# Queries and keys of the first spatial attention beside the end of the layers' last item, with the layers' pools on two sides of the memory

## The chip, the cores and the metric

The kernel runs on one core of a Trainium2 chip. The metric is device time in microseconds (us), the median of three runs. A core has five engines that each work through their own queue in order: TensorE (PE; its weight loads are PEld), VectorE (DVE), ScalarE (ACT), GpSimd (POOL) and SyncE (SP), which issues most of the DMAs. An engine that waits for a semaphore holds up everything behind it in its queue. SBUF holds the tiles the engines work on, PSUM the results of TensorE.

## The reference

The input is `x` of shape 2 x 128 x 64 x 64 in float32. Four blocks follow each other:

- **Layers.** A 1x1 embedding, two layers of layer norm, a selective state-space scan with gate, and a two-step feed-forward network with gelu, then a 1x1 output projection and the residual.
- **First spatial attention.** Queries, keys and values come from three 3x3 convolutions of the layers' output; softmax over all 4096 positions; a 1x1 projection; the residual.
- **Second spatial attention.** The same with 1x1 projections.
- **Multi-scale fusion.** 3x3 convolutions of the image at four scales, a small attention over the four scales at each pixel, a layer norm, and a fusion to 128 channels.

```python
q = conv2d(x, Wq, bq, 1).reshape(b, c, n)
k = conv2d(x, Wk, bk, 1).reshape(b, c, n)
v = conv2d(x, Wv, bv, 1).reshape(b, c, n)
attn = softmax(einsum('bci,bcj->bij', q, k) * scale, axis=2)
out = einsum('bij,bcj->bci', attn, v)
```

## The kernel before

The image lies in SBUF all the time as `xt`, with 128 channels on the partitions and both batches with a border of zeros. All blocks read it and write it back in place. Each block is a `with` body of its own that opens its tile pools at the start and closes them at the end. The order of the instructions on every engine is the order in which the Python code emits them (`tc.manual_schedule()`).

**Layers (L108 to L531).** The work is cut into `NI` = 32 items: 2 batches x 2 layers x 8 chunks of 512 positions, batch 0 first. An item has 32 slots. A loop runs `i` from -2 to 33, and in each slot it emits the scan's part (`spread_dt`, `spread_dtu`, `y_pair`, `scan`, `decay`, `times_b`, by groups of four slots, 256 groups in all) and then what `background(i)` lists for the slot. `background(i)` mixes four items at different stages: item `i+2` enters (embedding, first layer norm), `i+1` gets its projections, `i` its gate input, `i-1` ends its scan (`y_out` L407, `gate` L410, `mix_out` L416 to L420, second layer norm L222 to L278, `ffn_up` L429), and `i-2` ends with `gelu` L433, `ffn_down` L441 to L443, `ffn_add` L449 and L450, `out_mm` L455 and L456, `out_add` L460.

For `i` = 32 and 33 there is nothing left to scan after the slot 7 of item 32. What remains is the end of item 30 (L441 to L460) and the chain of the last item, 31: L407, L410, L416, L417, L420, L222 (centre), L229 (square), L236 (variance), L240 (`ve`), L244 to L247 (`rs`, `nt` on ScalarE), L252, L253, L257 (a Newton step on GpSimd and ScalarE), L261 (`pr`, the factor spread over the partitions), L265 (`cen`, on VectorE), L278 (`x2`, on ScalarE), L429 and L430 (four times), gelu, L441 to L460.

Pools of the layers: `l0w` (weights), `l0s` (all working tiles, among them five `h` tiles of 8 KB per partition, `bb`, `cb`, `dt`, `dtu`, `dtb`, `u`, `z`, `carry`), and in PSUM `l0mm` (2 banks), `l0bc` (1), `l0da` (4), `l0y` (1). `hid`, the feed-forward network's middle, uses the `h` tiles.

**First attention.** Runs `r` = 0 to 3 are (first, second attention) x (batch 0, 1). The pool `wbig` gets the weights `wa` (L539) and `uw`, a ring of three half filter sets (L573, 576 KB each) beside the tile `dlo`. The 3x3 convolutions of the first attention are computed in a transformed form. A batch's rows are cut into four chunks. For one chunk, `inputs` (L589 to L600) makes twelve VectorE combinations of shifted columns, eight into `dlo`, four into `dhi`; `products` (L612) multiplies them in six slots of three matmuls each into `pa` and `pb`; `outputs` copies two parts on ScalarE (L561, L620) and combines nine times on VectorE (L621 to L629). At the start of run 0 the queries of chunk 0 and the keys of all four chunks (`keys`) are made, in this order; then the loop over `now` begins, with scores (L706, taken up by VectorE's L711), exponentials (L721), transposes (L736), block copies and DMAs (L743, L745, L747) and products (L756).

A pool that is opened where closed pools lay waits, at its first uses, for the last user of those pools.

**Multi-scale.** It opens with the weights `ws` (L874), a few weight products (L890 to L907) and the image's means (L948).

Of the kernel before, what the change touches and what calls it, by code (L numbers as in the profile page):

```python
# [67 lines left out]
def tile_conv_seq(ctx: ExitStack, tc, x, consts, vecs, wemb, wlay, wconv, wdt, wqkv, wsmall, wms, out):  # L68
# [42 lines left out]
    with ExitStack() as s, tc.manual_schedule():  # L111
        wp = s.enter_context(tc.tile_pool(name="l0w", bufs=1))
        sp = s.enter_context(tc.tile_pool(name="l0s", bufs=1))
        mm = s.enter_context(tc.tile_pool(name="l0mm", bufs=2, space=PSUM))
        bc = s.enter_context(tc.tile_pool(name="l0bc", bufs=1, space=PSUM))
        dap = s.enter_context(tc.tile_pool(name="l0da", bufs=4, space=PSUM))
        yp = s.enter_context(tc.tile_pool(name="l0y", bufs=1, space=PSUM))
# [106 lines left out]
        def ln_square(w, k, i):  # L224
            if "sq" not in w:
                w["sq"] = sp.tile([P, 2, CH], F32, name="sq", tag="sq")
                w["cen"] = sp.tile([P, 2, CH], F32, name="cen", tag="cen")
            pc = w.pop(("pc", k))
            nc.scalar.activation(w["sq"][:, k, :], pc, AF.Square)  # L229
            nc.scalar.copy(w["cen"][:, k, :], pc)  # L230
# [7 lines left out]
        def ln_eps(w, n):  # L238
            w["ve"] = sp.tile([2, CH], F32, name="ve", tag="ve")
            nc.scalar.activation(w["ve"][:n], w.pop("var")[:n], AF.Identity, bias=eps[:n])  # L240

        def ln_rs(w, n):
            w["rs"] = sp.tile([2, CH], F32, name="rs", tag="rs")
            nc.scalar.activation(w["rs"][:n], w["ve"][:n], AF.Ln)  # L244
            nc.scalar.activation(w["rs"][:n], w["rs"][:n], AF.Exp, scale=-0.5)
            w["nt"] = sp.tile([2, CH], F32, name="nt", tag="nt")
            nc.scalar.activation(w["nt"][:n], w["rs"][:n], AF.Square)  # L247
# [19 lines left out]
        def ln_shift(w, k, i, second):  # L267
            if second:
                dst = st[i]["x2"] = sp.tile([P, CH], F32, name="x2", tag="x2")
# [26 lines left out]
        def pz_mm(i, j):  # L296
            if j == 0:
                st[i]["z"] = sp.tile([P, NJ, CH], F32, name="z", tag="z", bufs=2)
# [124 lines left out]
        def ffn_up(i, f):  # L423
            w = st[i]
            if f == 0:
                w["hid"] = sp.tile([P, 4, CH], F32, name="hid", tag="h", bufs=5)
# [18 lines left out]
        def ffn_add(i):  # L445
            b, l, c = items[i]
            if l == NL - 1:
                xr = st[i]["xr"] = sp.tile([P, CH], F32, name="xr", tag="xr")
# [65 lines left out]
        for i in range(-2, NI + 2):  # L514
            todo = background(i)
            for t_ in range(NSL):
                t = i * NSL + t_
                g, m = divmod(t, 4)
                if m == 0 and 0 <= g + 3 < NG:
                    spread_dt(g + 3)  # L520
                if m == 0 and 0 <= g + 1 < NG:
                    spread_dtu(g + 1)
                if m == 0 and g % 2 == 1 and 0 <= g - 3 < NG:
                    y_pair(g - 3)
                if 0 <= t < NT:
                    scan(t)
                if 0 <= t + 4 < NT:
                    decay(t + 4)
                if m == 3 and 0 <= g + 1 < NG:
                    times_b(g + 1)  # L530
                for f, a in todo[t_]:  # L531
                    f(*a)


    wbig = ctx.enter_context(tc.tile_pool(name="wbig", bufs=1))
    wa = wbig.tile([P, NWA], F32, name="wa")

    uw = wbig.tile([P, NS, 9, C], F32, name="uw", tag="wbig")
    nc.sync.dma_start(wa, wsmall[:, :NWA])  # L539
# [3 lines left out]
    QG = 256  # L543
    NB, NTH = P // 32, N // P // 2
    NU = 8 * N // QG
    LAG = 14
    with ExitStack() as s, tc.manual_schedule():
        sp = s.enter_context(tc.tile_pool(name="ats", bufs=1))
        pss = s.enter_context(tc.tile_pool(name="atps", bufs=2, space=PSUM))
        psa = s.enter_context(tc.tile_pool(name="atpa", bufs=2, space=PSUM))  # L550
        psm = s.enter_context(tc.tile_pool(name="atpm", bufs=1, space=PSUM))
        psq = s.enter_context(tc.tile_pool(name="atpq", bufs=1, space=PSUM))
# [5 lines left out]
        st = {}  # L558
# [11 lines left out]
        def load(which, half):  # L570
            slot = st["ring"] = (st.get("ring", -1) + 1) % 3
# [5 lines left out]
        def inputs(r, cc):  # L577

            dhi = st["dhi"] = sp.tile([P, 2, 18, 16], F32, name="dhi", tag="d")
# [23 lines left out]
        def products(which):  # L603
# [3 lines left out]
            for slot, dst in enumerate((pa[:, 2, :], pa[:, 0, :], pa[:, 3, :], pa[:, 1, :], pb[:, 0, :], pb[:, 1, :])):  # L607
                d = dlo[:, slot] if slot < 4 else st["dhi"][:, slot - 4]
                for y in range(3):
                    rhs = d[:, y : y + 16, :].rearrange("p h j -> p (h j)")  # L610
                    lhsT = uw[:, where[which, slot // 3], 3 * (slot % 3) + y, :]
                    nc.tensor.matmul(dst, lhsT=lhsT, rhs=rhs, start=(y == 0), stop=(y == 2))  # L612
            return pa, pb

        def outputs(pa, pb, dst, bias):

            tt, stt = nc.vector.tensor_tensor, nc.vector.scalar_tensor_tensor
            df = sp.tile([P, 2, QG], F32, name="df", tag="df")
# [37 lines left out]
        def keys(r):  # L656
            k = st["k"] = sp.tile([P, N], F32, name="k", tag="k")
            chunks(r, 1, lambda cc: k[:, cc * 4 * QG : (cc + 1) * 4 * QG])

        def values(r):  # L660
            vt = st["vt"] = sp.tile([P, N // P, C], F32, name="vt", tag="vt")
# [11 lines left out]
            def to(cc):  # L673
                if cc > 1:
                    turned(cc - 2)
                vs[cc] = sp.tile([P, 4 * QG], F32, name="vs", tag="tr", bufs=2)
# [6 lines left out]
        def queries(r, cc):  # L683

            for i in range(4):
                st["q", r, 4 * cc + i] = sp.tile([P, QG], F32, name="q", tag="q", bufs=5)
            outputs(*products(0), [st["q", r, 4 * cc + i] for i in range(4)], bias(r, 0))

        def query(r, grp):
            ps = psq.tile([P, QG], F32, name="pqq", tag="q")  # L690
            dense(r, 0, grp * QG, QG, ps)
            q = st["q", r, grp] = sp.tile([P, QG], F32, name="q", tag="q", bufs=5)
# [3 lines left out]
        def score(r, u):  # L696
            grp, w = divmod(u, 8)
            it, c2 = divmod(w, 4)
            if c2 == 0:
                st["mx"] = sp.tile([P, NCH // 2], F32, name="mx", tag="mx", bufs=2)  # L700
            if c2 % 2 == 0:
                st["sc", r, u // 4, c2 // 2] = sp.tile([P, N // 2], F32, name="sc", tag="sc", bufs=3)
            pq = pss.tile([P, 2, CH], F32, name="pq", tag="s")
            for i in range(2):
                at = (2 * c2 + i) * CH
                nc.tensor.matmul(  # L706
                    pq[:, i, :], lhsT=st["q", r, grp][:, it * P : (it + 1) * P], rhs=st["k"][:, at : at + CH], start=True, stop=True
                )
            at = c2 % 2 * 2 * CH
            dst = st["sc", r, u // 4, c2 // 2][:, at : at + 2 * CH].rearrange("p (a f) -> p a f", a=2)  # L710
            nc.vector.tensor_scalar(dst, pq, 1.0, None, ALU.mult, ALU.max, accum_out=st["mx"][:, c2 : c2 + 1])  # L711

        def exponentials(r, blk):
            scale = 1.0 if runs[r][0] else float(C) ** -0.5
            nm = sp.tile([P, 1], F32, name="nm", tag="nm", bufs=2)
            nc.vector.tensor_reduce(nm, st["mx"], AX.X, ALU.max)
            nc.vector.tensor_scalar(nm, nm, -scale, None, ALU.mult)  # L717
            sm = st["sm", r, blk] = sp.tile([P, 2], F32, name="sm", tag="sm", bufs=2)
            for hh in range(2):
                sc = st["sc", r, blk, hh]  # L720
                nc.scalar.activation(sc, sc, AF.Exp, bias=nm, scale=scale, accum_out=sm[:, hh : hh + 1])  # L721

        def turn(r, blk, hh):

            grp, it = divmod(blk, 2)
            if hh == 0:
                if it == 0:
                    st["rec", r, grp] = sp.tile([P, 2], F32, name="rec", tag="rec", bufs=2)
                rec = st["rec", r, grp][:, it : it + 1]
                nc.vector.tensor_reduce(rec, st.pop(("sm", r, blk)), AX.X, ALU.add)  # L730
                nc.vector.reciprocal(rec, rec)
            if it == 0:
                st["pt", r, grp, hh] = sp.tile([P, QG // 32, NTH, 32], F32, name="pt", tag="pt", bufs=4)
            pt = st["pt", r, grp, hh]
            tr = sp.tile([P, NB, NTH, 32], F32, name="tr", tag="tr", bufs=2)
            nc.vector.transpose(tr, st.pop(("sc", r, blk, hh)).rearrange("p (t r f) -> p r t f", r=NB, f=32))  # L736
# [13 lines left out]
        def product(r, u):  # L750
            grp, w = divmod(u, 8)
            if w == 0:
                st["po", r, grp] = psa.tile([P, QG], F32, name="po", tag="acc")
            for jt in range(4 * w, 4 * w + 4):
                rhs = st["pt", r, grp, jt // NTH][:, :, jt % NTH, :]
                nc.tensor.matmul(st["po", r, grp], lhsT=st["vt"][:, jt, :], rhs=rhs, start=(jt == 0), stop=(jt == N // P - 1))  # L756

        def diagonals(r, grp):
            for it in range(2):
                dg = st["dg", it] = sp.tile([P, P], F32, name="dg", tag="dg", bufs=2)  # L760
                nc.vector.tensor_scalar(dg, ident, st["rec", r, grp][:, it : it + 1], None, ALU.mult)

        def spread(r, grp):

            pr = psm.tile([P, QG], F32, name="pr", tag="m")
            for it in range(2):
                nc.tensor.matmul(pr[:, it * P : (it + 1) * P], lhsT=ones, rhs=st["dg", it], start=True, stop=True)
            rb = st["rb", r, grp] = sp.tile([P, QG], F32, name="rb", tag="rb", bufs=2)
# [10 lines left out]
        def divide(r, grp):  # L779
            on = st["on", r, grp] = sp.tile([P, QG], F32, name="on", tag="on")  # L780
            nc.vector.tensor_tensor(on, st.pop(("po", r, grp)), st.pop(("rb", r, grp)), ALU.mult)
# [3 lines left out]
        def finish_mm(r, grp):  # L785
            if not runs[r][0]:
                st["p2", r, grp] = psm.tile([P, QG], F32, name="p2", tag="m")
                nc.tensor.matmul(st["p2", r, grp], lhsT=wa[:, WS_O : WS_O + C], rhs=st["on", r, grp], start=True, stop=True)

        def finish(r, grp):  # L790
            if not runs[r][0]:
                nc.vector.scalar_tensor_tensor(xg(r, grp), st.pop(("p2", r, grp)).rearrange("p (h w) -> p h w", w=16), v1("bo1"), xg(r, grp), ALU.add, ALU.add)

        def at(f, u0):
# [7 lines left out]
        for which, half in ((0, LO), (0, HI), (1, LO)):  # L802
            load(which, half)
        for f in inputs(0, 0):
            f()
        queries(0, 0)
        load(1, HI)
        for now in range(NALL + LAG + 10):
            r, u = divmod(now, NU)
            w = now % 8  # L810
            if now < NALL:
                if u == 0:
# [3 lines left out]
                    keys(r)  # L816
# [29 lines left out]
            if w == 7:  # L846
                at(lambda r, u: finish_mm(r, u // 8), LAG + 9)
# [473 lines left out]
```

## Time and profile before

| | us |
|---|---|
| Runs: 5097.54, 5103.26, 5102.76; median | 5102.76 |
| The profiled execution's own time | 5104.57 |
| Its span, first to last instruction | 5102.8 |
| Layers until the last scan, in the span | 0 to 2102.5 |
| End of the layers' last items | 2102.5 to 2153.2 |
| Attention until its first score on VectorE | 2153.2 to 2206.0 |
| Attentions | 2206.0 to 4297.2 |
| Multi-scale | 4297.2 to 5102.8 |
| TensorE's mean granted clock | 0.946 |

The rows of the stretches are read from the engines' timelines. Over the whole span TensorE is busy 92%, VectorE 80%, ScalarE 46%, GpSimd 45%.

How to read the profile's lines: a timeline line has the start, the length, the engine, the line in the kernel, the operation, the output and the inputs by the names of the tiles, the shape and how often. What stands in brackets is the engine's idle time just before, and whose result ended it. A float32 matmul appears as two instructions, so three matmuls are six. The granted clock of TensorE is 1.00 at full speed.

### The profile page before, as it was taken

The page shows a single profiled execution, that of the slowest core. Times are in us where ns is not written, and L with a number is a line of the kernel's source. Part 1 is how long each engine was busy: PE and PEld are TensorE (multiplying, and loading weights), DVE is VectorE, ACT ScalarE, POOL GpSimd, SP SyncE. Part 2 cuts the span into 40 slices and gives each one's busy share as a digit, 9 for nine tenths or more (in the row PEclk, how much of TensorE's full clock was granted, in tenths as well). Part 3 has the DMA queues.
Part 4 walks back from the last instruction along what each step waited for, and adds up shares of the span by engine and source line. Part 5 has one row for each costly group of instructions (what it writes and reads, how often), then busy time and mean ns, then how long its engine had stood idle before and what let it go on. Part 6 is the DMA issues. An engine that isn't in the chain of part 4 may idle for free.

```text
span 5102.8 us, 48990 instructions
## 1 busy us (share of the span) xinstructions
PE 4686.2 (92%) x14797; PEld 2249.2 (44%) x14797; DVE 4094.2 (80%) x4416; ACT 2367.7 (46%) x3221; POOL 2317.8 (45%) x1948
## 2 busy tenths in 40 slices
PE   5888899899888998789999999999999998999997
PEld 1222222222222222256666666666666666333332
DVE  5999999999999999588888887667766775667775
ACT  4677777777777777412222232333333332323332
POOL 2777777666777777313332233333333332322331
PEclk8899998998999989899999999999999999999998
DMA  5333333332333333124443344444444443000000
GB/s 150 73 68 68 70 71 72 71 70 68 69 69 68 69 71 72 36 53 104 101 105 82 78 100 105 118 95 112 111 99 97 112 111 76 3 7 5 7 8 7
DMA packets 237016, 373.86 MB, mean 73 GB/s; under 512 B 88000, under 2 KB 88400, under 8 KB 228432
## 3 DMA queue, kind: packets, MB, share of 16 engines
q1 hardware_dynamic: 187600, 303.55, 25.0%
q10 hardware_dynamic: 49152, 67.17, 5.5%
q8 instruction: 118, 1.93, 0.2%
q14 instruction: 146, 1.20, 0.1%
HBM read 92.18 MB, written 9.83 MB: 20 GB/s over the span
## 4 chain that ended last, share of the span: by engine, by line
PE 46%; POOL 21%; DVE 13%; issue 11%; DMA 4%; ACT 3%; SPq 3%; DVEq 0%; ACTq 0%; POOLq 0%
POOL h L387 17%; PE po L756 13%; PE pq L706 13%; DVE tr L736 3%; DMA pt<-tr 2%; SPq L747 2%; PE pf L1008 2%; PE py L399 2%; PE pqkv L1035 2%; PE pw L1094 1%; POOL dtu L347 1%; POOL z L410 1%; PE pfus L1159 1%; PE pu L288 1%; PE psc L1059 1%
## 5 line engine op out<-in xcount | busy, mean ns | idle before, releaser
L743 POOL COPY pt<-tr 32x512 f32<-32x512 f32 x1024 | 657.8, 642 | 1496.0 <-DVE tr L736 769.0
L384 DVE TENSOR_TENSOR_SCAN h<-da,carry,h 128x512 f32<-128x512 f32 x1024 | 1240.9, 1265 | 60.1 <-ACT da L373 29.9
L387 POOL TENSOR_TENSOR h<-h,cb 128x2048 f32<-128x2048 f32 x256 | 1161.0, 4535 | 20.9 <-POOL carry L386 0.2
L706 PE MATMUL pq<-k,q 128*128 128x512 f32 x2048 | 966.5, 595 | 11.0 <-DVE sc L711 8.7
L756 PE MATMUL po<-pt,vt 128*128 128x256 f32 x4096 | 965.6, 379 | 2.5 <-DMA pt<-tr 2.5
L721 ACT ACTIVATE sc<-sc,nm 128x2048 f32<-128x2048 f32 x256 | 510.6, 1995 | 938.9 <-DVE nm L717 651.9
L711 DVE TENSOR_SCALAR_CACHE_REDUCE sc<-pq 128x1024 f32<-128x1024 f32 x512 | 625.0, 1222 | 361.3 <-PE pq L706 339.7
L756 PEld LDWEIGHTS po<-pt,vt 128*128 128x128 f32 x4096 | 777.9, 190 | 294.8 <-issue 211.4
L373 ACT ACTIVATE da<-dtb,am 128x512 f32<-128x512 f32 x1024 | 681.6, 684 | 223.8 <-DVE h L384 212.0
L736 DVE STREAM_TRANSPOSE tr<-sc 128x2048 f32<-128x2048 f32 x256 | 591.7, 2311 | 68.3 <-DMA pt<-tr 61.4
L366 DVE TENSOR_TENSOR h<-bb,pdu 128x2048 f32<-128x2048 f32 x256 | 581.3, 2271 | 78.4 <-PE py L399 29.4
L399 PE MATMUL py<-h,sel 128*32 128x512 f32 x2048 | 512.1, 644 | 1.6 <-POOL h L387 1.6
L706 PEld LDWEIGHTS pq<-k,q 128*128 128x128 f32 x2048 | 384.4, 191 | 291.3 <-issue 248.0
L360 PE MATMUL pdu<-dtu,fsel 128*128 128x512 f32 x512 | 324.3, 719 | 104.3 <-DVE h L366 104.2
L399 PEld LDWEIGHTS py<-h,sel 128*32 128x32 f32 x2048 | 115.4, 118 | 415.0 <-issue 407.9
L288 PE MATMUL pu<-xn,wu 128*128 128x512 f32 x512 | 246.1, 614 | 4.1 <-ACT xn L278 2.3
L360 PEld LDWEIGHTS pdu<-dtu,fsel 128*128 128x128 f32 x512 | 95.6, 213 | 309.8 <-DVE h L366 190.5
L386 POOL COPY carry<-h 128x4 f32<-128x4 f32 x256 | 47.8, 187 | 390.3 <-DVE h L384 386.4
L1101 DVE TENSOR_TENSOR ov<-v,pw 128x2048 f32<-128x2048 f32 x64 | 146.2, 2285 | 68.6 <-PE pw L1094 68.6
L1035 PE MATMUL pqkv<-f,ws 128*128 128x512 f32 x384 | 189.5, 618 | 3.0 <-DVE prod L1052 2.3
L1105 POOL TENSOR_TENSOR ov<-ov 128x2048 f32<-128x2048 f32 x16 | 72.6, 4537 | 257.6 <-DVE ov L1101 257.6
L261 PE MATMUL pr<-rs,kc 2*128 2x512 f32 (+1 forms) x128 | 90.2, 834 | 77.3 <-POOL rs L257 71.1
(241 smaller groups left out, 5331.8 us busy)
## 6 DMA issues: line engine op xcount, KB each, us to landing
pt<-tr SPq DMA_DIRECT2D x2048, 64.0 KB, 2.0
dtb<-dt SPq DMA_DIRECT2D x1024, 64.0 KB, 2.0
pt<-tr ACTq DMA_DIRECT2D x1024, 64.0 KB, 2.2
bb<-dr SPq DMA_DIRECT2D x128, 256.0 KB, 4.6
cb<-dr SPq DMA_DIRECT2D x128, 256.0 KB, 7.5
uw<-ufold SPq DMA_DIRECT2D x14, 576.0 KB, 3.9
xt<-in_x SPq DMA_DIRECT2D x16, 256.0 KB, 5.0
xr<-in_x SPq DMA_DIRECT2D x16, 256.0 KB, 2.9
```

The lines of the kernel that those rows point to most:

```text
L360: nc.tensor.matmul(pdu, lhsT=four(s_ % 4), rhs=st[i]["dtu"][:, s_ // 4, :], start=True, stop=True)
L366: nc.vector.tensor_tensor(h, st[i]["bc", 0], pdu.unsqueeze(1).to_broadcast([P, 4, CH]), ALU.mult)
L373: nc.scalar.activation(da, st[i]["dtb", s_], AF.Exp, scale=am[items[i][1]][:, j, gg, m : m + 1])
L384: nc.vector.tensor_tensor_scan(h[:, m, :], da, h[:, m, :], carries[b, l][:, j, gg, m : m + 1], ALU.mult, ALU.add)
L387: nc.gpsimd.tensor_tensor(h, h, st[i]["bc", 1], ALU.mult)
L399: nc.tensor.matmul(py[r : r + 32, :], lhsT=sel, rhs=st[i]["h", s_ + k][:, m, :], start=(m == 0), stop=(m == 3), tile_position=(0, r),)
L706: nc.tensor.matmul(pq[:, i, :], lhsT=st["q", r, grp][:, it * P : (it + 1) * P], rhs=st["k"][:, at : at + CH], start=True, stop=True)
L711: nc.vector.tensor_scalar(dst, pq, 1.0, None, ALU.mult, ALU.max, accum_out=st["mx"][:, c2 : c2 + 1])
L721: nc.scalar.activation(sc, sc, AF.Exp, bias=nm, scale=scale, accum_out=sm[:, hh : hh + 1])
L736: nc.vector.transpose(tr, st.pop(("sc", r, blk, hh)).rearrange("p (t r f) -> p r t f", r=NB, f=32))
L743: nc.gpsimd.tensor_copy(dst, src)
L756: nc.tensor.matmul(st["po", r, grp], lhsT=st["vt"][:, jt, :], rhs=rhs, start=(jt == 0), stop=(jt == N // P - 1))
```

## The change

- The pools of the layers are cut in two. `l0w`, a new pool `l0t` (`sq`, `cen`, `ve`, `rs`, `nt`, `x2`, `z`, `xr`), `l0mm` and `l0y` stay on the left side of the memory and are closed at the end of the layers. The rest, `l0s`, `l0bc` and `l0da`, lies on the right side and is closed after slot 7 of item 32.
- The slot's body becomes a function `slot`. After slot 7 of item 32, `wbig`, `ata` (the attention's `dhi`, `q`, `k`, `df`, `sc`, `tr` and small tiles) and the PSUM pools `atps`, `atpq` are opened on the right side.
- The attention's beginning becomes a generator, `beginning`, which stops after the inputs and after each of the six slots of products. In slots 8 to 31 of item 32 it is advanced by the digits of `beside`, ahead of the slot's own work: 19 steps, from the loads and inputs of chunk 0 to the products of the keys' chunk 1. What is left of it runs after the layers' last slot.
- In those slots the order on the queues is: four slots of the queries' products and the weight loads ahead of `out_mm` of item 30 and L222 of item 31; a fifth ahead of L236; the sixth, the six of the keys' chunk 0 and three of chunk 1 ahead of L261; two more ahead of L429's first; the sixth of chunk 1 between L429's second and third.
- `hid` of the last item is taken from the score tiles of `ata`.
- `wbig`, the attention's pools and the multi-scale pools are opened with `reuse_waits="tile"`: a tile waits for the users of the old tiles that lay where it lies.
- `keys(0)` is no longer called in the loop. The attention's dictionary `st` is renamed `sta`, and `at` in its loop `in_turn`.

```diff
-    with ExitStack() as s, tc.manual_schedule():
-        wp = s.enter_context(tc.tile_pool(name="l0w", bufs=1))
-        sp = s.enter_context(tc.tile_pool(name="l0s", bufs=1))
...
+    layers, scans = ctx.enter_context(ExitStack()), ctx.enter_context(ExitStack())
+    with tc.manual_schedule(), ExitStack() as s:
+        wp = layers.enter_context(tc.tile_pool(name="l0w", bufs=1))
+        spl = layers.enter_context(tc.tile_pool(name="l0t", bufs=1))
+        mm = layers.enter_context(tc.tile_pool(name="l0mm", bufs=2, space=PSUM))
+        yp = layers.enter_context(tc.tile_pool(name="l0y", bufs=1, space=PSUM))
+        sp = scans.enter_context(tc.tile_pool(name="l0s", bufs=1, side="right"))
+        bc = scans.enter_context(tc.tile_pool(name="l0bc", bufs=1, space=PSUM, side="right"))
+        dap = scans.enter_context(tc.tile_pool(name="l0da", bufs=4, space=PSUM, side="right"))
...
             if f == 0:
-                w["hid"] = sp.tile([P, 4, CH], F32, name="hid", tag="h", bufs=5)
+                if i == NI - 1:
+                    w["hid"] = spa.tile([P, 4, CH], F32, name="hid", tag="sc", bufs=3)
+                else:
+                    w["hid"] = sp.tile([P, 4, CH], F32, name="hid", tag="h", bufs=5)
...
-        for i in range(-2, NI + 2):
+        for i in range(-2, NI):
             todo = background(i)
             for t_ in range(NSL):
...
+                slot(i, todo, t_)
+        todo = background(NI)
+        for t_ in range(8):
+            slot(NI, todo, t_)
+        scans.close()
+        wbig = ctx.enter_context(tc.tile_pool(name="wbig", bufs=1, side="right", reuse_waits="tile"))
...
+        spa = s.enter_context(tc.tile_pool(name="ata", bufs=1, reuse_waits="tile", side="right"))
+        pss = s.enter_context(tc.tile_pool(name="atps", bufs=2, reuse_waits="tile", space=PSUM, side="right"))
+        psq = s.enter_context(tc.tile_pool(name="atpq", bufs=1, reuse_waits="tile", space=PSUM, side="right"))
...
+        def beginning():
+            for which, half in ((0, LO), (0, HI), (1, LO)):
+                load(which, half)
+            for f in inputs(0, 0):
+                f()
+            yield
+            for i in range(4):
+                sta["q", 0, i] = spa.tile([P, QG], F32, name="q", tag="q", bufs=5)
+            pp = yield from products_by(0)
+            outputs(*pp, [sta["q", 0, i] for i in range(4)], bias(0, 0))
+            load(1, HI)
+            k = sta["k"] = spa.tile([P, N], F32, name="k", tag="k")
+            for cc in range(NCC):
+                pp = yield from products_by(1)
+                ahead = inputs(0, cc + 1) if cc + 1 < NCC else []
+                for f in ahead[:8]:
+                    f()
+                at = cc * 4 * QG
+                outputs(*pp, [k[:, at + i * QG : at + (i + 1) * QG] for i in range(4)], bias(0, 1))
+                for f in ahead[8:]:
+                    f()
+        steps = beginning()
+        beside = '2111001000112111111011010000'
+        for k in range(8, 2 * NSL):
+            if k == NSL:
+                todo = background(NI + 1)
+            for _ in range(int(beside[k - 8]) if k - 8 < len(beside) else 0):
+                next(steps, None)
+            slot(NI + k // NSL, todo, k % NSL)
+        for _ in steps:
+            pass
+        layers.close()
+        sp = s.enter_context(tc.tile_pool(name="ats", bufs=1, reuse_waits="tile"))
+        psa = s.enter_context(tc.tile_pool(name="atpa", bufs=2, reuse_waits="tile", space=PSUM))
+        psm = s.enter_context(tc.tile_pool(name="atpm", bufs=1, reuse_waits="tile", space=PSUM))
...
-                    keys(r)
+                    if r:
+                        keys(r)
...
-        sp = s.enter_context(tc.tile_pool(name="mss", bufs=1))
-        mm = s.enter_context(tc.tile_pool(name="msmm", bufs=3, space=PSUM))
+        sp = s.enter_context(tc.tile_pool(name="mss", bufs=1, reuse_waits="tile"))
+        mm = s.enter_context(tc.tile_pool(name="msmm", bufs=3, reuse_waits="tile", space=PSUM))
```

`products_by` is `products` with a `yield` after each of the six slots.

## The prediction

> **What bounds the kernel around the change.** I first read the busy table by stage, then each engine's timeline from 2084 to 2226 us. The last scan of the layers ends near 2102.5, the last item is finished at 2153.2, and the first score reaches VectorE at 2206. Busy time in these stretches (columns: stretch, length, busy of PE, PEld, DVE, ACT and POOL, granted TensorE clock, DMA share, GB/s):
>
> ```profile
> 2102.50:2153.20 50.70, 35.49 (x70) 12.14 (x68) 3.08 (x5) 22.18 (x26) 9.55 (x5) 0.79 0.03 7
> 2153.20:2206.00 52.80, 45.08 (x187) 36.92 (x188) 44.24 (x92) 3.68 (x10) 0.00 (x0) 0.94 0.21 71
> ```
>
> In the first stretch VectorE works 3 of 51 us: one item's dependent steps run through TensorE, ScalarE and GpSimd in turn. In the second VectorE works 44 of 53 us and is the bound. VectorE's timeline gives the borders (start, length, line; idle before it and its releaser in brackets):
>
> ```profile
> 2111.04 0.75 DVE L407 SCALAR_TENSOR_TENSOR u<-u,vec,py 128x512 f32<-128x512 f32 x1 [8.57 <-PE py L399]
> 2130.68 0.75 DVE L265 SCALAR_TENSOR_TENSOR cen<-cen,vec,pr 128x512 f32<-128x512 f32 x1 [18.89 <-PE pr L261]
> 2151.58 0.68 DVE L589 SCALAR_TENSOR_TENSOR uw<-xt 128x288 f32<-128x288 f32 x1 [20.16 <-PE po L455]
> ...
> 2184.43 0.41 DVE L621 TENSOR_TENSOR k<-df,pa 128x256 f32<-128x256 f32 x1
> ...
> 2205.95 1.22 DVE L711 TENSOR_SCALAR_CACHE_REDUCE sc<-pq 128x1024 f32<-128x1024 f32 x1
> ```
>
> L589 needs only the finished batch 0, yet waits 20 us for the last item. L621 at 2184.43 is the first output step of the keys' chunk 1 (of 0 to 3).
>
> **What leaves the path.** The new order puts the queries, the keys' chunk 0 and the products of chunk 1 into the tail; the outputs of chunk 1, and chunks 2 and 3, stay behind it, since their ScalarE copies (L561, L620) are queued after the last item's L460. So behind the tail remain 0.8 us of copies and L621 (2184.43) to the first score (2205.95), 21.5: together 22.3. Before, the end of L460 (2153.19) to the score took 52.8. That takes 30.5 us out, if the tail itself were not delayed.
>
> **What the tail pays.** Its instructions now stand in the same in-order queues as the inserted ones.
>
> TensorE. One step is three matmuls. Warm, twelve take 2166.54 to 2171.72, so a step is 1.30:
>
> ```profile
> 2110.93 3.70 PE L441 MATMUL pf<-hid,wl 128*128 128x512 f32 x8
> ...
> 2142.52 6.26 PE L441 MATMUL pf<-hid,wl 128*128 128x512 f32 x8 [4.00 <-ACT hid L433]
> ...
> 2166.54 5.34 PE L612 MATMUL pa<-uw 128*128 128x256 f32 x24
> 2171.72 2.75 PE L612 MATMUL pb<-dhi,uw 128*128 128x256 f32 x12
> ```
>
> Four query steps stand ahead of L222 (start 2119.62, then 2124.8), a fifth ahead of L236 (2121.33, then 2127.0: +5.6). The ten further steps (sixth of the queries, six of chunk 0, three of chunk 1) stand ahead of L261 and end near 2141.0.
>
> ScalarE. The queries' two copies (0.85) come between L240 and L244. They end at 2129.7, and the tail's rs is ready near 2135, not 2128.5. That is earlier than L261 can start (2141.0), so it costs nothing.
>
> VectorE sets this part. From 2129.7 it has, ahead of L265: outputs of the queries 3.9 (as L621 2184.43 to L597 2188.31), eight inputs of chunk 1 4.3 (2169.25 to 2173.59), outputs of chunk 0 3.9, four inputs 2.6 (2188.31 to 2190.90): 14.7, so L265 could start at 2144.4. The first twelve inputs (7.1) run from 2111.8 to 2118.9 in VectorE's idle time; without that cover they would be 7.1 more.
>
> Now a rule against this change. The tail's two GpSimd products (L252, L257, 1.25 each) will run beside VectorE instructions with two SBUF inputs. The trace shows that conflict: L590 alone at the start (x4), and in the main loop beside GpSimd's copies (x18), min/median/max in ns:
>
> ```profile
> L590 DVE SCALAR_TENSOR_TENSOR uw<-xt x4: 658/675/676, 2152.2 to 2191.5; 128x288 f32<-128x288 f32 x4
> ```
> ```profile
> L590 DVE SCALAR_TENSOR_TENSOR uw<-xt x18: 672/1108/1144, 2221.3 to 3117.6; 128x288 f32<-128x288 f32 x18
> ```
>
> The Trainium skill (SBUF — State Buffer, section "SBUF: two separate sides") says that VectorE with two SBUF inputs and a GpSimd instruction that reads SBUF share a port pair as an exclusive lock: the first holds it for its whole instruction. By the rule two GpSimd products cost VectorE up to 2.5. By the row a copy of 0.61 (L743's median) costs 0.43, some 70%: 2 x 1.25 x 0.7 = 1.7. I take 1.7 (bounds 0 and 2.5). L265 starts at 2146.1 instead of 2130.68: +15.4.
>
> From there: L278 0.75 later, L429 at 2147.65. The four eliminations of hid ended 7.0 after L429 before (2132.23 to 2139.25, cold) and 6.3 in the item before (2099.73 to 2106.0, half cold). Warm, with one step inserted, I take 5.7: 2153.3. Table load and gelu 3.2: 2156.5.
>
> Then L441 to L460 of the last item. TensorE idles 3.9 there (last elimination 0.69 and 3.2), as before (4.00). The granted clock (third column from the end) shows what such a gap did:
>
> ```profile
> 2138.60:2140.50 1.90, 0.00 (x0) 0.00 (x0) 0.00 (x0) 1.88 (x2) 0.00 (x0) 1.00 0.00 0
> 2140.50:2142.50 2.00, 0.00 (x0) 0.00 (x0) 0.00 (x0) 1.97 (x3) 0.00 (x0) 0.59 0.00 0
> 2142.50:2144.00 1.50, 1.48 (x2) 0.84 (x3) 0.00 (x0) 1.27 (x1) 0.00 (x0) 0.50 0.00 0
> ```
>
> Clock 1.00, then half, and L441 took 6.26 instead of 3.70. The Trainium skill (TensorE: Matmul & The Clock Gate, "What's actually happening") has a free-running window of about 3.4 us, one idle window halving the clock. A gap of 3.9 need not hold a whole window, so the rule leaves warm likelier. The row, and L612's 8.02 after 3.69 idle, were cold both times; I take cold: gelu's end to L460's end 10.7 (2142.47 to 2153.19), so the tail ends at 2167.2, +14.0. Warm would be 2.6 less (L441's difference).
>
> The first score then comes at 2167.2 + 22.3 = 2189.5, a gain of **16.4** (30.5 - 14.0).
>
> **Queues and memory.** SP now issues wa and three weight loads ahead of xr of item 30. They wait until the scan pool's memory underneath is free. The profile doesn't tell which tiles lie there: between the last carry copy (2102.7) and GpSimd's L410 (reads u until 2114.2). Early costs nothing: wa's issue to the first products took 4.5 (2151.58 to 2156.09), the four loads drained in 6.5, and xr lands near 2112, before L456 wants it (2124). Late costs 3.4: weights at 2118.7 instead of TensorE being free at 2115.3, and everything behind waits with it. I take early, as the latest scan tiles are freed by 2102.7 and the wait is now per tile. load(1,HI) waits for the first three query steps; behind it on SP only xr of item 31, needed after 2160. hid of the last item in the score buffers costs nothing: these are unused until 2189.
>
> **Entry of the last stage.** The per-tile wait also applies to the multi-scale pools:
>
> ```profile
> 4301.22 0.30 PE L890 MATMUL pwt<-kc,ws 128*128 128x128 f32 x1 [5.08 <-DMA ws<-in_wsmall]
> ```
>
> The load of ws was issued at 4297.37, after the attention's last VectorE instruction, though SP issued its last other transfer by 4286.3. If ws's memory is free by then, L890 starts at 4296.2 when TensorE ends its products; L907 follows 3.46 later as before (4301.22 to 4304.68), VectorE's own work ahead ends near 4300.1, and L948 starts near 4300.2, not 4304.81: **4.6**. If its memory is read by the last products, ws lands 1 us earlier only, gain 1; if it waits as a pool, 0. I take 4.6: in first-use order the pool begins with the transposed weights' first buffer, last read before 4280.
>
> **Sum.** The layers before 2111 and the main loops keep their order and move as they are. The profiled execution took 5104.57 with span 5102.8; its span is at the median of the runs, 5102.76. 16.4 + 4.6 = 21.0, so 5102.8 - 21.0 = **5082**. A measurement of this kernel tells some 0.2% (10 us) from no change.
>
> **Rivals.**
> - *Cheaper tail* (16%). Warm L441 (-2.6) and no port conflict (-1.7) give 5077.5; a tail not delayed at all gives 5102.8 - 30.5 - 4.6 = 5067.7. For it: TensorE is busy almost all the time until 2146. Against: VectorE's 14.7 must precede L265. Place: 5067 to 5077.
> - *Late hand-over* (15%). The new pools wait for the whole scan pool: 3.4 lost in the tail, 4.6 not gained, 5090; with further stalls up to 5096. For it: both stages' openings waited for the old pools' last user before (L589 for L455, ws for L783). About a third of it lies within 0.2%.
> - *It does nothing* (6%): the inserted work delays the tail by all 30 us, for instance because L265 waits for more of chunk 1 than listed. 5093 to 5103.
> - *Slower by placement* (5%). Every layer tile gets another address. If that made the scan loop's 256 groups 0.12 us longer each, the 31 us would turn the gain into a loss of 10, 5113; from 0.08 per group the gain is gone. Against: L387 takes 4.52 to 4.55 in all buffers in the stretch read, L384 1.255 to 1.282.
>
> **Numbers.** The forecast itself has 58%, 5077 to 5088. Below 0.2% faster: 0.58 + 0.16 + 0.11 = 0.85; within 0.10; slower 0.05. The range 5073 to 5093 leaves out half of the cheaper tail (0.07), the end of the hand-over, and the last two cases (0.13).
>
> **What would show it.** Right: L589's first instruction at 2112; L265 near 2146; L441 of the last item about 6.3 long; L460's end near 2167; the first L711 near 2190; ws issued before 4290. Wrong: L612's first matmul waiting for uw's load after 2116 (hand-over), long idle stretches of VectorE between 2130 and 2146 (another wait is the bound), or group lengths of L387 other than 4.5 (placement).

## The result and the profile after

The changed kernel took **5077.70 us** (median of 5 runs, 5074.78 to 5081.85). The kernel before took 5100.63 beside it (5 runs, 5097.54 to 5103.26). The ratio is **0.9954**, with a 95% interval of 0.9942 to 0.9967: 22.9 us faster, where 21.0 had been forecast. (The 5082 on record was counted from the profiled span of 5102.8; from 5100.63 the same gain leads to 5079.6.) The profiled execution has a span of 5075.9 against 5102.8, which is 26.9 less; the 4 us beyond the medians are accounted for below.

Busy time by stretch, with the borders now set at the end of the last scan (2102.9), the end of the last item (2167) and the first score (2189). Columns as before: stretch, length, busy of PE, PEld, DVE, ACT and POOL, granted clock, DMA share, GB/s:

```profile
2102.90:2167.00 64.10, 56.07 (x183) 32.08 (x182) 30.35 (x53) 23.47 (x31) 10.29 (x5) 0.97 0.16 54
2167.00:2189.00 22.00, 17.91 (x76) 13.55 (x74) 20.32 (x43) 2.06 (x6) 0.00 (x0) 1.00 0.09 28
```

The tail is 13 us longer than it was, but VectorE works 30 us in it instead of 3, and the granted clock is 0.97 instead of 0.79. What stays behind the tail is 22 us instead of 53.

VectorE's timeline gives the borders:

```profile
2111.47 0.75 DVE L411 SCALAR_TENSOR_TENSOR u<-u,vec,py 128x512 f32<-128x512 f32 x1 [8.56 <-PE py L403]
...
2112.72 2.85 DVE L600 SCALAR_TENSOR_TENSOR uw<-xt 128x288 f32<-128x288 f32 x1
...
2130.32 0.42 DVE L640 TENSOR_TENSOR q<-df,pa 128x256 f32<-128x256 f32 x1 [8.99 <-ACT df L639]
...
2132.62 1.37 DVE L645 TENSOR_TENSOR q<-q 128x256 f32<-128x256 f32 x1
...
2134.82 0.42 DVE L648 TENSOR_TENSOR q<-q,pb 128x256 f32<-128x256 f32 x1
2135.16 1.31 DVE L599 SCALAR_TENSOR_TENSOR uw<-xt 128x288 f32<-128x288 f32 x1
...
2146.60 0.75 DVE L269 SCALAR_TENSOR_TENSOR cen<-cen,vec,pr 128x512 f32<-128x512 f32 x1
...
2167.62 0.42 DVE L640 TENSOR_TENSOR k<-df,pa 128x256 f32<-128x256 f32 x1 [15.93 <-ACT df L639]
...
2189.13 1.22 DVE L730 TENSOR_SCALAR_CACHE_REDUCE sc<-pq 128x1024 f32<-128x1024 f32 x1
```

L599 (from 2112.13) and L600 are the first two inputs of chunk 0 (L589 and L590 before), and L269 is the last item's centring (L265 before). From L640 at 2130.32 to L269 VectorE has no idle time: its own list of work decides when the tail goes on. It then idles 15.93 until the last item has passed, because ScalarE's copy L639 for chunk 1 stands in ScalarE's queue behind the item's L467.

GpSimd's timeline shows what three of those VectorE lines met:

```profile
2112.30 2.73 POOL L414 TENSOR_TENSOR z<-z,u 128x1024 f32<-128x1024 f32 x1 [4.54 <-DVE u L411]
```
```profile
2132.22 1.49 POOL L256 TENSOR_TENSOR nt<-nt,ve 1x512 f32<-1x512 f32 x1 [17.19 <-ACT nt L251]
2134.54 1.37 POOL L261 TENSOR_TENSOR rs<-rs,nt 1x512 f32<-1x512 f32 x1 [0.83 <-ACT nt L257]
```

Each of L600, L645 and L599 (2135.16) starts while one of these runs, and each is longer than its like: 2.85, 1.37 and 1.31 where 0.67, 0.42 and 0.67 are usual. All three read two tiles or views in SBUF. L648 starts while L261 runs as well, but its second input, `pb`, lies in PSUM, and it takes its usual 0.42.

SP's queue shows when the new pools handed over their memory, and TensorE's timeline how the last item went on:

```profile
2103.19 1.28 SPq L583 DMA_DIRECT2D uw<-ufold  x3
```
```profile
2142.04 1.12 PE L265 MATMUL pr<-rs,kc 1*128 1x512 f32 x2
...
2157.15 5.40 PE L448 MATMUL pf<-hid,wl 128*128 128x512 f32 x8 [4.00 <-ACT hid L440]
```

The weights were requested at 2103.19, when the last carry was copied, and xr right behind them (2104.51). L448 waited 4.00 for hid, as before, and took 5.40, between the warm 3.70 and the 6.26 of the kernel before.

The entry of the last stage, SP's queue and then VectorE's timeline:

```profile
4264.64 0.52 SPq L926 DMA_DIRECT2D ws<-in_wsmall  x1
```
```profile
4276.36 0.49 DVE L802 SCALAR_TENSOR_TENSOR xt<-on,vec,xt 128x256 f32<-128x256 f32 x1
...
4277.17 0.63 DVE L934 COPY spread<-spr 128x128 f32<-128x128 f32 x4
...
4278.33 2.28 DVE L1000 TENSOR_TENSOR t<-xt 128x2048 f32<-128x2048 f32 x1
```

The load of ws went out 12 us before the attention's last VectorE instruction (L802). That instruction's start to the first mean (L1000) is now 1.97; before it was 8.12 (4296.69 to 4304.81).

### The profile page after: what moved, and what is told of

Its sections match the earlier page's. It is cut to its first block, busy times and chain, and to the rows that moved or that the text cites. A ratio compares the mean times of both kernels' runs of the same rounds, so it can differ in the third digit from the quotient of the medians.

```text
span 5075.9 us, 48999 instructions
## 1 busy us (share of the span) xinstructions
PE 4683.8 (92%) x14797; PEld 2250.9 (44%) x14797; DVE 4097.5 (81%) x4416; ACT 2366.9 (47%) x3221; POOL 2316.3 (46%) x1948
## 4 chain that ended last, share of the span: by engine, by line
PE 47%; POOL 21%; DVE 13%; issue 11%; DMA 3%; ACT 3%; SPq 2%; ACTq 0%; DVEq 0%; POOLq 0%
POOL h L391 16%; PE po L775 13%; PE pq L725 13%; DVE tr L755 3%; DMA pt<-tr 2%; PE pf L1060 2%; SPq L766 2%; PE py L403 2%; PE pqkv L1087 2%; PE pu L292 1%; PE pw L1146 1%; POOL dtu L351 1%; PE pfus L1211 1%; POOL z L414 1%; PE psc L1111 1%
## 5 line engine op out<-in xcount | busy, mean ns | idle before, releaser
L351 POOL TENSOR_TENSOR dtu<-dt,u 128x1024 f32<-128x1024 f32 x32 | 75.0, 2345 | 189.7 <-ACT dt L345 189.7
```

## Experiments

My theory: the start gains some 16 us, since work moved into VectorE's idle time outweighs the delay of the tail; the entry of the last stage gains about 6 by its own mechanism, the per-tile wait; the two add up. Rivals: the new placement of the layers' tiles alone changes the time, and the moved steps earn little beyond what the per-tile waits give. The kernel before took 5101.32 (30 runs) beside the first four kernels and 5101.75 (7 runs) beside the last three.

**1. The entry alone**: the kernel before, with per-tile waits on the four multi-scale pools.

```diff
-        sp = s.enter_context(tc.tile_pool(name="mss", bufs=1))
-        mm = s.enter_context(tc.tile_pool(name="msmm", bufs=3, space=PSUM))
+        sp = s.enter_context(tc.tile_pool(name="mss", bufs=1, reuse_waits="tile"))
+        mm = s.enter_context(tc.tile_pool(name="msmm", bufs=3, reuse_waits="tile", space=PSUM))
...
```

> The kernel before with per-tile waits on the four multi-scale pools alone. Theory (two separate gains): the load of ws is issued before the attention's last products end, and the first means start about 6 us earlier than before (the changed kernel's profile shows 1.5 from the attention's last VectorE instruction to the means, before 7.6). The layers and the first score stay where they were (first score at 2206). Total -6, about 5095. Rival (the entry's gain belongs to the new places of the pools, not to the wait): nothing, 5101.

It took 5095.78 (20 runs), ratio 0.9988 (0.9982 to 0.9995): 5.5 less. SP's queue, then VectorE:

```profile
4284.87 0.53 SPq L874 DMA_DIRECT2D ws<-in_wsmall  x1
```
```profile
4294.95 0.49 DVE L783 SCALAR_TENSOR_TENSOR xt<-on,vec,xt 128x256 f32<-128x256 f32 x1
...
4296.93 2.28 DVE L948 TENSOR_TENSOR t<-xt 128x2048 f32<-128x2048 f32 x1
```

L783 to L948 is 1.98, as in the changed kernel. The entry needs nothing of the rest of the change.

**2. The change without the entry**: the changed kernel with the four multi-scale pools as they were.

```diff
-        sp = s.enter_context(tc.tile_pool(name="mss", bufs=1, reuse_waits="tile"))
-        mm = s.enter_context(tc.tile_pool(name="msmm", bufs=3, reuse_waits="tile", space=PSUM))
+        sp = s.enter_context(tc.tile_pool(name="mss", bufs=1))
+        mm = s.enter_context(tc.tile_pool(name="msmm", bufs=3, space=PSUM))
...
```

> The changed kernel with pool-wide waits on the multi-scale pools again. Theory: first score at 2189 as in the changed kernel, the entry 6 us longer, ws issued only after the attention's last VectorE instruction: 5078 + 6 = 5084. Rival (the whole gain is the beginning beside the tail): 5078.

It took 5085.70 (6 runs), ratio 0.9968 (0.9957 to 0.998): 15.6 less than before. SP's queue and VectorE:

```profile
4279.02 0.34 SPq L926 DMA_DIRECT2D ws<-in_wsmall  x1
```
```profile
4278.34 0.49 DVE L802 SCALAR_TENSOR_TENSOR xt<-on,vec,xt 128x256 f32<-128x256 f32 x1
...
4279.33 1.83 DVE L934 COPY spread<-spr 128x128 f32<-128x128 f32 x4
...
4286.63 2.28 DVE L1000 TENSOR_TENSOR t<-xt 128x2048 f32<-128x2048 f32 x1
```

The load again leaves after L802, and L802 to L1000 is 8.29. Experiments 1 and 2 together give 5.5 + 15.6 = 21.1 of the 22.9: the two parts add up within what medians of 5 to 30 runs tell.

**3. Nothing beside the tail**: the changed kernel, its pools and waits as they are, with all steps left behind the last item.

```diff
-        beside = '2111001000112111111011010000'
+        beside = ''
```

> The changed kernel with no step beside the tail: the whole beginning is put after the last item. Same pools, same places. Theory: the tail ends near 2153 again; the loads and the first twelve inputs still run before, as they wait per tile only, and the queries' products follow warm, so their copies start near 2158 instead of 2164, first score near 2199; with the entry's 6 about 5088. Rival one (the interleaving earns nothing, the per-tile waits all of it): 5078. Rival two (the new places of the pools slow the loops): the scan loop longer than 2102.5 or the attention longer than 2091, and more than 5090.

It took 5088.49 (9 runs), ratio 0.9976 (0.9966 to 0.9986): 12.8 less than before. VectorE's timeline, then TensorE's:

```profile
2129.51 0.75 DVE L269 SCALAR_TENSOR_TENSOR cen<-cen,vec,pr 128x512 f32<-128x512 f32 x1 [18.89 <-PE pr L265]
2130.18 0.67 DVE L599 SCALAR_TENSOR_TENSOR uw<-xt 128x288 f32<-128x288 f32 x1
...
2157.21 0.42 DVE L640 TENSOR_TENSOR q<-df,pa 128x256 f32<-128x256 f32 x1 [20.05 <-ACT df L639]
```
```profile
2150.21 1.02 PE L463 MATMUL po<-xr,kc 128*128 128x512 f32 x2
2151.06 5.34 PE L622 MATMUL pa<-uw 128*128 128x256 f32 x24
```

The tail is not delayed here, as it should be. But the start is already 6.6 shorter: the tail ends at 2152.0 and the first output of the queries starts 5.2 later; before it was 11.85 (2153.19 to 2165.04). Since the pools no longer wait for the layers' last user, VectorE makes its inputs during the tail (2130.18 on, in program order behind L269), the weights are there, and TensorE goes from L463 into the products without a pause, at 5.34 instead of 8.02. With 6.15 for the entry that is 12.8, as the medians have it (the profiled span is 16.1 shorter: the layers ended 1.2 earlier too, the attention was 3.1 shorter, and what follows the entry 0.9 longer). So of the start's gain **6.6 are the pools' waits** and the rest of it, some 10, is the moving of the steps. The 6.6 come from two things together, the pools on the other side of the memory and the per-tile waits; no run tells them apart. The placement rival falls: the scan loop runs as in the kernel before, each group 1.1 to 1.2 earlier from the first to the last. The attention is not slower either (2087.6 from the first score to L802, before 2090.7).

**4. The port conflict**: the changed kernel without the last item's Newton step. It leaves out L256, L261 and a ScalarE instruction between them, so that item's normalisation is coarser.

```diff
         def ln_newton(w, n):
...
+            if w.get("last"):
+                return
             nc.gpsimd.tensor_tensor(nt, nt, w["ve"][:n], ALU.mult)
...
         def ln_step(w, n):
             rs = w["rs"][:n]
+            if w.get("last"):
+                return
             nc.gpsimd.tensor_tensor(rs, rs, w["nt"][:n], ALU.mult)
...
-            w, m = {}, len(pair)
+            w, m = {"last": i == NI}, len(pair)
```

> The changed kernel without the Newton step of the last item's second layer norm: its two GpSimd products and the ScalarE step between them are left out. Theory (port conflict): the two long VectorE instructions of the beginning (1.37 instead of 0.42 and 1.31 instead of 0.67) return to their lengths, and the last item's scaling on VectorE starts 1.6 earlier, near 2145.0, with TensorE's spread before it still at 2142. Rival (the step sets the chain because the spread waits for it): the spread starts more than 2 us earlier.

One run: 5077.66, span 5075.9. VectorE's timeline (its L649, L603 and L273 are L645, L599 and L269 above), then TensorE's (its L269 is the spread, L265 above, and its L452 is L448):

```profile
2132.55 0.42 DVE L649 TENSOR_TENSOR q<-q 128x256 f32<-128x256 f32 x1
...
2134.15 0.68 DVE L603 SCALAR_TENSOR_TENSOR uw<-xt 128x288 f32<-128x288 f32 x1
...
2144.97 0.75 DVE L273 SCALAR_TENSOR_TENSOR cen<-cen,vec,pr 128x512 f32<-128x512 f32 x1
```
```profile
2141.97 1.12 PE L269 MATMUL pr<-rs,kc 1*128 1x512 f32 x2
...
2155.52 6.75 PE L452 MATMUL pf<-hid,wl 128*128 128x512 f32 x8 [4.00 <-ACT hid L444]
```

Both instructions are back at 0.42 and 0.68 and the centring is 1.6 earlier, while the spread starts at 2141.97 as before (2142.04): the GpSimd products cause the 1.6, and the rival falls. The end doesn't show it, because the four matmuls (eight instructions) behind the same 4.00 of waiting took 6.75 instead of 5.40: 1.35 of the 1.6 went there.

**5. TensorE kept busy in the gap**: four matmuls whose result nobody reads, between the up-projections and L448.

```diff
             slot(NI + k // NSL, todo, k % NSL)
+            if k == NSL:
+                keep = yp.tile([P, CH], F32, name="keep", tag="y")
+                for _ in range(4):
+                    nc.tensor.matmul(keep, lhsT=ident, rhs=st[NI - 1]["x2"], start=True, stop=True)
```

> The changed kernel with four extra matmuls (their result is read by nobody) on TensorE between the last item's up-projections and its gelu, so that TensorE doesn't idle 4 us there. Theory (clock): the eight matmuls of L448 behind the gelu take 3.7 instead of 5.4 (6.3 in the kernel before), the tail ends 1.7 earlier, near 2165.3, and the first score comes near 2187.4 instead of 2189.1. Rival (the clock isn't the cause of the slow L448): it stays over 5.

One run: 5071.86, span 5070.1. TensorE's timeline:

```profile
2150.51 3.60 PE L856 MATMUL keep<-x,kc 128*128 128x512 f32 x8
2154.67 3.70 PE L448 MATMUL pf<-hid,wl 128*128 128x512 f32 x8 [0.57 <-ACT hid L440]
...
2179.56 4.54 PE L622 MATMUL pb<-dhi,uw 128*128 128x256 f32 x12 [2.31 <-DVE dhi L608]
```

L448 is warm, 1.7 saved. But the first score came at 2186.64, and its layers had ended 2.5 earlier than the changed kernel's: no gain at all. The products of chunk 3 lost it: after 2.31 of waiting they took 4.54, where the changed kernel took 2.86 after the same wait (2183.72). Windows around them show the granted clock (third from the end):

```profile
2176.37:2179.79 3.42, 1.11 (x6) 0.65 (x5) 3.28 (x8) 0.73 (x2) 0.00 (x0) 1.00 0.54 172
2179.79:2183.20 3.41, 3.41 (x9) 2.70 (x9) 2.31 (x5) 0.00 (x0) 0.00 (x0) 0.50 0.00 0
```

The clock was halved for 3.41 us and cost 1.7 of them. In this run, then, the filled gap gained 1.7 and a later one took it back; the part on the prediction below shows what decides which gap pays. The 5.8 us by which this span is below the changed kernel's are mostly the layers (2.5), which lie ahead of the edit, and the attention (1.4 at the borders of its runs, 1.7 in its last block of matmuls).

**6. Real work in the gap**: more of the beginning ahead of L448, the outputs of chunk 1 and the first four slots of products of chunk 2. (These are four more advances of the generator, as the digits show, not five as the expectation has it.)

```diff
-        beside = '2111001000112111111011010000'
+        beside = '2111001000112111111011011111'
```

> The changed kernel with five more steps of the beginning (outputs of the keys' chunk 1, four product slots of chunk 2) put between the last item's up-projections and its gelu's use. Theory (what is left behind the tail costs its full length, and VectorE idles 16 us there): 11 us of VectorE work move into that idle time, the tail ends about where it did (later by the two ScalarE copies and one step, earlier by a warm clock), first score near 2178, time 5067. Rival (the tail is the bound, and anything added to it costs as much as it moves): 5078.

It took **5064.68** (4 runs), ratio 0.9927 (0.9911 to 0.9944). TensorE's timeline, then VectorE's:

```profile
2151.83 5.34 PE L622 MATMUL pa<-uw 128*128 128x256 f32 x24
2157.01 3.60 PE L448 MATMUL pf<-hid,wl 128*128 128x512 f32 x8
```
```profile
2153.38 0.42 DVE L640 TENSOR_TENSOR k<-df,pa 128x256 f32<-128x256 f32 x1 [2.84 <-ACT df L639]
...
2177.14 1.22 DVE L730 TENSOR_SCALAR_CACHE_REDUCE sc<-pq 128x1024 f32<-128x1024 f32 x1
```

L448 starts at 2157.01, in the changed kernel at 2157.15 (1.0 later if counted from the end of the layers), warm and with no wait. ScalarE makes chunk 1's copies ahead of the gelu, so VectorE's 15.93 of idle time shrink to 2.84, and the first score comes 12.0 earlier, of which 1.2 is the layers.

**7. Finer steps**: the generator cut into pieces of one product, one set of copies, outputs and inputs each; ScalarE's copies come right after the fourth product, and the tail's centring is ahead of the second half of chunk 1's inputs. Nearly all of the beginning lies beside the tail.

```diff
+                for s_ in range(4):
+                    one(s_)
+                    yield
...
+                put(df[:, 0, :], pa[:, 0, :], b_)
+                nc.scalar.copy(df[:, 1, :], pa[:, 1, :])
...
+                yield
+                for s_ in (4, 5):
+                    one(s_)
+                    yield
...
-        beside = '2111001000112111111011010000'
+        beside = {8: 2, 9: 1, 10: 1, 11: 1, 12: 1, 14: 1, 18: 2, 19: 1, 20: 2, 21: 3, 22: 1, 23: 2, 29: 3, 30: 3, 31: 2, 32: 3, 33: 2, 34: 3, 36: 1, 40: 4, 42: 20}
...
-            for _ in range(int(beside[k - 8]) if k - 8 < len(beside) else 0):
+            for _ in range(beside.get(k, 0)):
```

> The changed kernel with the beginning cut into finer steps and nearly all of it put beside the tail: the queries' copies before the fifth product slot, the last item's scaling on VectorE ahead of the four second inputs of chunk 1, chunks 2 and 3 in the gaps of the feed-forward network, chunk 3's outputs ahead of the last output projection. Theory: TensorE is the bound, 30 steps of 1.3 and 17 us of the tail from 2116: first score near 2173, time 5062. Rival (the tail's dependent steps are the bound): the last item's scaling starts later than 2147, first score after 2185, 5074 or more.

It took **5062.15** (4 runs), ratio 0.9922 (0.9907 to 0.9936), and beats both kernels: 39.6 us under the kernel before. A window from L240 to the first score, and VectorE's timeline:

```profile
2126.00:2172.72 46.72, 46.63 (x183) 33.94 (x182) 40.40 (x79) 15.67 (x24) 2.52 (x2) 1.00 0.09 27
```
```profile
2141.57 0.74 DVE L269 SCALAR_TENSOR_TENSOR cen<-cen,vec,pr 128x512 f32<-128x512 f32 x1
...
2172.72 1.23 DVE L730 TENSOR_SCALAR_CACHE_REDUCE sc<-pq 128x1024 f32<-128x1024 f32 x1 [0.84 <-PE pq L725]
```

From 2126 to the first score TensorE is busy 46.63 of 46.72 us and the clock is full: TensorE is now the bound of this part, and the tail's dependent steps are hidden. Counted from the end of the layers, the first score comes 14.8 earlier than in the changed kernel and 4.0 earlier than in experiment 6; the medians of 6 and 7 differ by 2.5, and the intervals of their ratios overlap.

## Why the prediction was right

**Where the 26.9 of the two profiled executions lie.** The layers ended 0.43 later. From there to the first score 17.25 were gained (2205.95 to 2189.13 is 16.8, and the 0.43); predicted 16.4. The attention from the first score to its last VectorE instruction was 3.5 shorter; predicted 0. The entry gained 6.15; predicted 4.6. The rest gained 0.4. Together 17.25 + 3.5 + 6.15 + 0.4 - 0.43 = 26.9. The medians saw 22.9. Two of these terms, the layers and the attention, wander from run to run by a few us (below), and the profiled execution of the kernel before was one of its slower ones (5104.57).

**Hand-over.** "Early" held: loads from 2103.19, xr at 2104.51, L463 never waited. Experiment 3 shows what the waits alone are worth, 6.6; the prediction had this inside its 30.5 and had not told it apart from the moved work.

**VectorE sets the tail.** Predicted: outputs from 2129.7, 14.7 of work, 1.7 of conflict, L265 at 2146.1. Measured: 2130.32, 16.28 in all, 2146.60. TensorE's pr came at 2142.04 (2141.0 predicted), so it was VectorE that held the tail, as argued.

**The port conflict** was 0.95 + 0.64 = 1.6, against 1.7 by the row and 2.5 by the rule; experiment 4 shows its cause. The number came out by the row, but the traces bear out the rule of the Trainium skill (SBUF — State Buffer, "SBUF: two separate sides"): the VectorE instruction waits for the rest of the GpSimd instruction that began first. That rest is 1.09 for L645 (2132.62 to 2133.71), 0.75 for L599 (2135.16 to 2135.91) and 2.31 for L600 (2112.72 to 2115.03); the three instructions were longer by 0.95, 0.64 and 2.18. So the 2.5 of the rule was a worst case, with VectorE arriving just after GpSimd, and the 70% was luck. I also overlooked that L600 would meet L414: 2.2, lost in VectorE's idle time.

**The cold L448 is the mis-sized term of the tail**: 6.26 taken, 5.40 measured. hid was complete at 2153.88 (2153.3 predicted) and L467 ended at 2166.97 (2167.2): +13.35 against the layers' shift, where +14.0 was predicted. From there to the score 0.65 of copies and 21.51 followed; 22.3 was predicted. "Cold" was right as to the clock; what was taken over unchanged was how long it stays low. The changed kernel's windows, then the kernel before's:

```profile
2151.56:2154.97 3.41, 1.59 (x4) 0.38 (x2) 0.13 (x1) 2.45 (x3) 0.00 (x0) 1.00 0.00 0
2154.97:2158.38 3.41, 1.23 (x3) 0.68 (x4) 0.00 (x0) 3.38 (x3) 0.00 (x0) 1.00 0.00 0
2158.38:2161.80 3.42, 3.42 (x5) 1.33 (x4) 0.00 (x0) 0.02 (x1) 0.00 (x0) 0.50 0.00 0
```
```profile
2140.88:2147.70 6.82, 5.18 (x6) 2.18 (x7) 0.00 (x0) 2.87 (x2) 0.00 (x0) 0.50 0.00 0
```

The clock is at 1.00 or at 0.50, and it is low for 3.41 us in one kernel and 6.82 in the other. The four matmuls take 3.70 and half of the low time that falls on them: 3.70 + 3.42 / 2 = 5.41 (5.40 measured), before 3.70 + 5.18 / 2 = 6.29 (6.26), and in experiment 4, with 6.18 low, 6.79 (6.75). In the stretches read (2090 to 2230, 3740 to 3860 and 4200 to 4300 of every trace) the clock falls and rises only at whole multiples of 3.413 us from one another: in the changed kernel its falls at 3769.47 and 4260.99 come 472 and 616 such steps after the one at 2158.38. The prediction could not know where on this grid the wait of 4.00 would lie: it was as long as before, but it lay otherwise. That is the free-running window of the Trainium skill (TensorE: Matmul & The Clock Gate, "What's actually happening"), 3413 ns there. The prediction read the rule as asking for a window that is idle throughout. In the windows read here the clock fell after those with TensorE busy 1.39 us or less and stayed at 1.00 after those with 1.59 or more, so a wait well under a window can be enough (2.31 in experiment 5).

**The entry** is mis-sized by 1.5. The step "VectorE's own work ahead ends near 4300.1" copied the old durations. Before, GpSimd's memsets for this stage waited for the pool too and ran beside VectorE's copies (VectorE, then GpSimd, kernel before):

```profile
4297.68 1.84 DVE L882 COPY spread<-spr 128x128 f32<-128x128 f32 x4
```
```profile
4297.93 1.73 POOL L951 MEMSET xs<- 128x1156 f32 x3
```

With per-tile waits most of the memset work ran at 4260.8, and the four copies took 0.63. Experiment 2 has 1.83 with the pool wait back, experiment 1 has 0.63 without it. That is 1.2 of the 1.5. The weights' matmuls no longer hold the end at all.

**The attention's 3.5** was not in the sum, and it isn't the change's. The transposes move against those of the kernel before almost only at the borders of the attention's runs, in all by -5.2, and the attention's last block of matmuls takes 1.7 longer. TensorE's timeline at the border of run 3 and in the last block, kernel before, then changed kernel:

```profile
3787.09 6.58 PE L634 MATMUL pp<-xt,wa 128*128 128x512 f32 x8 [3.40 <-ACT k L561]
...
4282.09 14.05 PE L756 MATMUL po<-pt,vt 128*128 128x256 f32 x64 [2.46 <-DMA pt<-tr]
```
```profile
3768.08 5.40 PE L653 MATMUL pp<-xt,wa 128*128 128x512 f32 x8 [3.43 <-ACT k L571]
...
4260.07 15.74 PE L775 MATMUL po<-pt,vt 128*128 128x256 f32 x64 [2.43 <-DMA pt<-tr]
```

The same waits, and other durations after them, in both directions. It is the grid again: at the border of run 3 the clock was low from 3786.10 to 3792.93 before and from 3769.47 to 3772.89 in the changed kernel; in the last block it was never low before and low from 4260.99 to 4264.41 after. At two other borders it was low for 3.41 before (from 2765.5 and from 3366.3) and stays at 1.00 in the changed kernel, whose transposes come 1.65 and 1.42 earlier there. The term isn't a property of the code: experiment 2, with the changed kernel's attention code, takes 2090.6 from the first score to L802, the kernel before 2090.7 and the changed kernel 2087.2.

**The rivals.** The late hand-over and "it does nothing" are refuted by SP's queue and by experiment 2, and placement by experiment 3. The cheaper tail came partly true by L448's 0.86.

## What to carry to other kernels

Look first for what a stage's opening waits for as a whole: here the pools' waits, without any moved work, held 6.6 us at the start and 6.15 at the end, and both showed as a transfer or an instruction that starts only after the previous stage's last one. When work is laid beside a dependent chain, write out the list of each in-order engine up to the chain's next instruction; here VectorE's list, 16.3 us, set the tail's delay. More steps laid beside the tail brought the first score another 10.8 us nearer to the end of the layers (experiment 6), a finer order 14.8 (experiment 7). The gap of 4 us on TensorE was best filled with work that is needed anyway; work without use there saved 1.7 at once and, in its one run, lost it at a later gap.

## What the runs showed of the hardware

- A VectorE instruction with two SBUF inputs that starts during a GpSimd product waits for that product's rest, within 0.14: 2.85 instead of 0.67 in the longest case. One with its second input in PSUM didn't (0.42 as ever). Four small copies on VectorE took 1.84 and 1.83 beside GpSimd memsets, 0.63 where most of these ran earlier.
- Around TensorE's waits of 2.3 to 4.0 us read here its granted clock was 1.00 or 0.50, and it changed only on a grid of 3.413 us: down after a window with TensorE busy 1.39 us or less, up again one or two windows later. So four matmuls (eight instructions) of 128x512 took 5.40 to 6.75 behind 3.40 to 4.00 of waiting. Waits of 2.3 to 2.5 cost as well where one window held them: 4.54 instead of 2.86 behind 2.31 in experiment 5, and 15.74 instead of 14.05 for 32 matmuls (64 instructions) behind 2.43 in the changed kernel.
- The layers, whose instructions keep their order in all kernels, ended between 2.06 earlier and 0.43 later than in the kernel before; in experiment 1, whose layers are unchanged, 1.63 earlier. A difference of 2 us between two profiles needs its stage before it means anything.
